# GpSimd's order in the last stage, the drain of attention, and the low parts of the feed-forward's weights: one change to a four-layer conditioned kernel

## Chip, cores and metric

The kernel runs on one core of a Trainium2 chip. Times are microseconds of device time. The kernel before was run three times; its time is their median. A profiled execution of it, taken by the hardware profiler, gives the page and the trace; its own time lies a little beside the median, and both are given below. A core has five engines that work at the same time, each through its own queue of instructions in a fixed order: TensorE (matmuls; PE, with PEld for its weight loads), VectorE (DVE), ScalarE (ACT), GpSimd (POOL) and SyncE (SP), which here only issues DMAs. GpSimd issues some DMAs too.

## The reference

`x` is 64 samples of 64 tokens with 256 features, `cond` 64 samples of 64 features. Four layers follow one another:

```python
# L0: norm with a scale from cond, gated up projection, int8 values times ternary weights
h = x * (scale(cond) * rsqrt(mean(x*x) + 1e-6))
val, gate = split(h @ up_w.T)                      # 2 x 1024
x = x + act_quant(val * gelu(gate)) @ weight_quant(down_w).T
# L1: attention (16 heads of 16), then SwiGLU; gamma, beta, alpha are made from cond
x = x + a_alpha * attention(a_gamma * rms(x) + a_beta)
n = f_gamma * rms(x) + f_beta
x = x + f_alpha * ((silu(n @ gate_w.T) * (n @ hidden_w.T)) @ out_w.T + out_b)
# L2: layernorm, with tanh of a projection of cond added
x = (layernorm(x) * weight + bias + tanh(lin(cond))) * weight + bias
# L3: a bottleneck of 128 whose two weight matrices are made for each sample from cond
Wd_b = Wd + 0.1 * (cond @ Wdd.T + bdd);  Wu_b = Wu + 0.1 * (cond @ Wdu.T + bdu)
x = x + relu(x @ Wd_b.T + bd) @ Wu_b.T + bu
```

The change touches the feed-forward of L1 (SwiGLU), L2 and L3, and the way into them from the attention.

## The kernel before

**Stages.** The 4096 tokens are cut into 8 blocks (`NBLK`) of 512 tokens, 8 samples each. Stage 1 (about 20 to 272 us of the trace) does L0 for all blocks and makes the per-sample parts of L3's weights, which GpSimd's DMAs store in DRAM (`s1d`, `s2d`). Stage 2 (273 to 465 us) does the attention in 16 half blocks `w` and stores its result `x2` in DRAM. Stage 3 does the feed-forward, L2 and L3 in one loop (lines 1003 to 1028). Between stages 2 and 3 lies a stretch written out by hand, the drain of attention (lines 971 to 991): the last half block's weighing and projection among the first products of the feed-forward.

**Products in parts.** A product in fp32 is done as three fp32r matmuls (`mm3`, lines 83 to 85): high part by high part, high by low, low by high. The high part is a rounded copy by ScalarE; the low part is the value minus the high part, by VectorE or GpSimd. Weights are taken apart as well: a `Splitter` (lines 168 to 189) loads a slice, ScalarE copies the high part (L187), VectorE subtracts (L188). One of them takes the attention's weights in stage 1, a second one, made at line 896, takes the feed-forward's in stage 2, 16 slices in all, one or two for each `w` from 1 to 13 (lines 953 to 956).

**The loop of stage 3.** Step `n = 8i + f` handles slice `f` of the hidden layer (128 of 1024) for block `i`:
- `f_inner(n)`: TensorE's products for gate and hidden values (`gh` banks), Silu by ScalarE (L689), their product `sg` by VectorE (L690);
- `f_parts(n)`: the high part `hhi` by ScalarE (L709), the low part `hlo` by VectorE (L710);
- `f_outer(n-2)`: TensorE's product of slice `n-2` with the output weights, into the `acc` banks;
- at `f == 1`, `f_residual(i-1)` closes the block before: two products with alpha (L734), two sums with `x2` (which holds the bias already), called `fx` in the trace (L737), statistics (L739, L740), the root `rs_ln` on GpSimd (L200, L202) and four scalings on VectorE (L743). Then `f_weights(i-1)` loads the adapters' weights `wd` and `wu` on SyncE's queue (L753, L756) and adds the part that is common to all samples with four GpSimd sums of 128x1024 (L759);
- at `f == 3`, `f_rows(i)` loads alpha and bias rows on SyncE and adds the bias to `fx` with two GpSimd sums (L673); `f_start(i+1)` loads the next block's `x2`, squares it on ScalarE (L209), takes its root `rs_f` on GpSimd (L200, L202), and normalises it with four VectorE instructions (L223) into `xnf`;
- at `f` 5 and 6, `f_norm(i+1)`: TensorE transposes (L230), VectorE multiplies by gamma (L233, `xg`), GpSimd adds beta (L234), ScalarE copies the high part (`xhf`), GpSimd subtracts for the low part (L217, `xlf`);
- at `f` 4 to 7, `f_adapt` (transposes L769, L2's weights L770), `f_down` (L780) and `f_up` (L794, L796) do L2's end and L3 for block `i-1`.

`f_last` (from L799) does the last block's end in two halves.

**What sets the order.** Up to line 992, `manual_schedule` (line 92) holds TensorE, ScalarE, VectorE and GpSimd to the order of the source. At 992 `ordered.close()` ends that, and from there the language's scheduler decides where an instruction stands in its engine's queue. SyncE's queue is not in the manual list. Buffers set the rest: two banks in PSUM for `mm`, two for `acc`, four for `gh`; two `st` tiles (used by `sg` and by the Splitter), three `oh`/`ol` tiles (`hhi`/`hlo`), four each of `wd` and `wu`, one of the alpha rows.

**The drain.** Slices 0 to 2 of block 0 were multiplied during the attention's last two half blocks and parked in SBUF (`f_keep`, `room`, lines 693 to 697). In the drain `f_kept(n)` (line 699) applies Silu (L701) and the product, `f_parts` takes the parts, and `f_outer(0)` to `f_outer(3)` use them.

Of the kernel before, what the change touches and what calls it, by code (L numbers as in the profile page):

```python
# [8 lines left out]
F32 = mybir.dt.float32  # L9
# [8 lines left out]
P = 128  # L18
# [18 lines left out]
def tile_kernel(ctx: ExitStack, tc, xT, x, condT, cw, upT, downT, qkvT, woT, ghT, outT_w,  # L37
# [130 lines left out]
    class Splitter:  # L168


        def __init__(self, *jobs):
            self.todo = [(hi, lo, src.rearrange("(c p) n -> p c n", p=P), c, slice(j, j + step))
                         for hi, lo, src, kc, n, step in jobs for c in range(kc) for j in range(0, n, step)]
            self.there = []
# [9 lines left out]
        def turn(self):  # L184
            if self.there:
                hi, lo, st = self.there.pop(0)
                nc.scalar.copy(hi, st)  # L187
                nc.vector.tensor_tensor(lo, st, hi.bitcast(F32), ALU.subtract)  # L188
            self.load()

    def two(pool, name, kc, n):
# [402 lines left out]
    def a_weigh(w):  # L594

        i, tp = w // 2, w % 2
        pool = pools["b"]
        U = units.pop(w)
        pts, rp = U["pts"], U["rp"]
        po, vb = bank("po"), ablk[i]["vb"]  # L600
        for u in range(2):
            for m in range(2):
                for h in range(2):
                    o = (2 * u + m) * P + h * 64
                    for j in range(4):
                        nc.tensor.matmul(po[32 * j:32 * (j + 1), o:o + 64],  # L606
                                         lhsT=vb[:, 2 * tp + u, h, 4 * m + j, :], rhs=pts[j // 2][:, j % 2, o:o + 64],
                                         start=True, stop=True, tile_position=(0, 32 * j))
        of = pool.tile([P, 512], F32, tag="of", bufs=1, name=f"of{w}")
        nc.scalar.copy(of, po)  # L610
        pr = bank("mm")
        for a in range(4):
            nc.tensor.transpose(pr[:, a * P:(a + 1) * P], rp[:, 8 * a:8 * a + 8].rearrange("p h d -> p (h d)"), ident)
        nc.vector.tensor_tensor(of, of, pr, ALU.mult)
        units[w, "f"] = of
# [50 lines left out]
    def f_rows(i):  # L666

        fblk[i]["at"] = load_rows(1, "alpha", i)
        ab = load_rows(2, "ab", i)
        x2 = fblk[i]["x2"]  # L670
        for tp in range(TT // 2):
            s = slice(2 * tp, 2 * tp + 2)
            nc.gpsimd.tensor_tensor(x2[:, s], x2[:, s], ab[:, s], ALU.add)  # L673
# [12 lines left out]
    def f_inner(n):  # L686
        pg, pv = f_products(n)
        sg = main.tile([P, T], F32, tag="st", bufs=2, name=f"sg{n}")
        nc.scalar.activation(sg, pg, AF.Silu)  # L689
        nc.vector.tensor_tensor(sg, pv, sg, ALU.mult)  # L690
        return sg

    def f_keep(n):
# [2 lines left out]
        nc.scalar.copy(room[n][:, 0], pg)  # L696
        nc.vector.tensor_copy(room[n][:, 1], pv)

    def f_kept(n):
        g, v = room[n][:, 0], room[n][:, 1]  # L700
        nc.scalar.activation(g, g, AF.Silu)  # L701
        nc.vector.tensor_tensor(g, v, g, ALU.mult)
        return g

    def f_parts(n, sg):
        pool = pools["b"]
        h_hi = pool.tile([P, T], F32R, tag="oh", bufs=3, name=f"hhi{n}")
        h_lo = pool.tile([P, T], F32R, tag="ol", bufs=3, name=f"hlo{n}")
        nc.scalar.copy(h_hi, sg)  # L709
        nc.vector.tensor_tensor(h_lo, sg, h_hi.bitcast(F32), ALU.subtract)  # L710
        fun[n] = (h_hi, h_lo)

    def f_outer(n):
        i, f = divmod(n, 8)
        h_hi, h_lo = fun.pop(n)
        wout = pools["wout"]
        if f == 0:
            fblk[i]["acc"] = [bank("acc") for _ in range(2)]
        acc = fblk[i]["acc"]
        for t in range(TT):  # L720
            ts = slice(t * P, (t + 1) * P)
            mm3(acc[t // 2][:, (t % 2) * D:(t % 2 + 1) * D], (h_hi[:, ts], h_lo[:, ts]),
                (wout[0][:, f], wout[1][:, f]), f == 0 and t % 2 == 0, f == 7 and t % 2 == 1)
# [22 lines left out]
    def f_weights(i):  # L746
        pool = pools["c"]
        fblk[i]["wd"], fblk[i]["wu"] = [], []
        for k in range(2):
            bs = slice(i * BB + 4 * k, i * BB + 4 * k + 4)  # L750
            wd = pool.tile([P, 4, 2, BN], F32, tag="wd", bufs=4, name=f"wd{i}_{k}")
            for c in range(2):
                nc.sync.dma_start(out=wd[:, :, c, :], in_=s1d[c, bs].rearrange("b d n -> d b n"))  # L753
            wu = pool.tile([P, 4, D], F32, tag="wu", bufs=4, name=f"wu{i}_{k}")
            for s in range(2):
                nc.sync.dma_start(out=wu[s * 64:(s + 1) * 64], in_=s2d[s, bs].rearrange("b n d -> n b d"))  # L756
            bias = pools["bias"]
            for w, row in ((wd.rearrange("p b c n -> p b (c n)"), bias[:, 0]), (wu, bias[:, 1])):
                nc.gpsimd.tensor_tensor(w, w, row.unsqueeze(1).broadcast_to([P, 4, D]), ALU.add)  # L759
            fblk[i]["wd"].append(wd)  # L760
            fblk[i]["wu"].append(wu)

    def f_adapt(i, c):
        B = fblk[i]
# [97 lines left out]

    vx = pools["vx"] = pools["kv"].tile([P, TT, 2, 8, 32], F32, name="vx")
    nc.gpsimd.memset(vx, 0.0)
    splits = Splitter((qkv[0], qkv[1], qkvT, 2, 3 * D, 256), (wo[0], wo[1], woT, 2, D, 256))

    hooks = {3: [cond_load], 4: [cond_rest], 7: [splits.load]}
    for n in range(8, 16):
# [24 lines left out]
    pools["tags"] = dict(S=1, mm=4)  # L893
    pools["gh"] = two(fw, "gh", 2, 2 * FF)
    pools["wout"] = two(fw, "wout", 8, D)
    splits = Splitter((*pools["gh"], ghT, 2, 2 * FF, 512), (*pools["wout"], outT_w, 8, D, 256))
    splits.load()
    N = NBLK * 8
    W = 2 * NBLK
# [14 lines left out]
    for w in range(W):  # L914
        i, tp = divmod(w, 2)
        todo = [lambda k=k: a_ahead(i + 1, k) for k in ((2, 3, 4) if tp == 0 else (5, 6, 7))]
        if i + 1 == NBLK:
            if tp == 0:
                room = rooms()
            todo = [lambda: f_keep(0), lambda: f_keep(1)] if tp == 0 else [lambda: f_keep(2), lambda: a_turn(w, 0)]  # L920
            todo.append(lambda: None)
        a_score(w)
        a_shift(w, 0)
        if w > 0:
            a_weigh(w - 1)
        a_shift(w, 1)
        if tp == 1:
            ablk[i]["at"] = load_rows(0, "alpha", i)
            if i + 3 < NBLK:
                a_load(i + 3)  # L930
            elif i + 3 == NBLK:
                f_load(0)
        if tp == 0:
            if i + 2 < NBLK:
                a_scale(i + 2)
            elif i + 2 == NBLK:
                f_scale(0)
        a_exp(w, 0)
        if w > 0:
            a_parts(w - 1)  # L940
        todo[0]()
        a_sum(w, 0)
        todo[1]()
        a_exp(w, 1)
        todo[2]()
        for rest in late:
            rest()
        late = []
        if tp == 0 and i + 2 <= NBLK:
            late = [a_norm_turn(i + 2, c) for c in range(2)]  # L950
        a_sum(w, 1)
        if w > 0:
            a_project(w - 1)
        a_recip(w)
        if 1 <= w < 14:
            splits.turn()
            if w % 4 == 0:
                splits.turn()
        if w < W - 1:
            a_turn(w, 0)  # L960
            a_turn(w, 1)
            a_rows(w)
        if tp == 1:
            if i + 3 < NBLK:
                a_begin(i + 3)
            elif i + 3 == NBLK:
                f_begin(0)
# [4 lines left out]
    a_rows(W - 1)  # L972
    s0 = f_kept(0)
    f_parts(0, s0)
    s1 = f_kept(1)
    f_parts(1, s1)
    s3 = f_inner(3)
    a_weigh(W - 1)
    s2 = f_kept(2)
    a_parts(W - 1)  # L980
    f_outer(0)
    f_outer(1)
    f_parts(2, s2)
    f_parts(3, s3)
    a_project(W - 1)
    f_rows(0)
    f_start(1)
    s4 = f_inner(4)
    f_outer(2)
    f_parts(4, s4)  # L990
    f_outer(3)
    ordered.close()
    side.close()


# [7 lines left out]
    for n in range(5, N + 2):  # L1003
        i, f = divmod(n, 8)
        if n < N:
            f_parts(n, f_inner(n))
        if n == N:
            f_weights(NBLK - 1)
        if n > 5:
            f_outer(n - 2)  # L1010
        if f == 1 and 0 < i < NBLK:
            f_residual(i - 1)
            f_weights(i - 1)
        if i == NBLK:
            continue
        if f == 3:
            f_rows(i)
            if i + 1 < NBLK:
                f_start(i + 1)
        if i + 1 < NBLK and f in (5, 6):  # L1020
            f_norm(i + 1, f - 5)
        if i > 0:
            if f in (4, 5):
                f_adapt(i - 1, f - 4)
            if f == 6 and i + 1 < NBLK:
                f_down(i - 1)
            if f == 7 and i + 1 < NBLK:
                f_up(i - 1)
    f_last(NBLK - 1)


# [53 lines left out]
```

## Time and profile before

| what | value |
|---|---|
| median of 3 runs (lowest, highest) | 799.27 us (797.81, 801.54) |
| the profiled execution's own time | 794.82 us |
| its span, first to last instruction | 793.0 us |
| mean granted TensorE clock | 0.994 |
| TensorE busy, 20 to 272 us (stage 1) | 250.16 of 252.00 us |
| TensorE busy, 273 to 465 us (stage 2) | 178.93 of 192.00 us |
| TensorE busy, 465 to 495 us (block 0 of stage 3) | 29.37 of 30.00 us |
| TensorE busy, 495 to 515 us | 14.39 of 20.00 us |
| TensorE busy, 515 to 790 us (rest of stage 3) | 268.70 of 275.00 us |
| GpSimd busy, 495 to 515 us; 515 to 790 us | 19.83 of 20.00 us; 124.38 of 275.00 us |

How to read it: busy times add the lengths of an engine's instructions in a stretch; what an engine lacks to the stretch's length is time in which it waited or issued. The clock is the share of full speed that TensorE was granted. In lines of the trace, `L710 DVE TENSOR_TENSOR hlo<-sg,hhi 128x512` is an instruction of VectorE from line 710 that writes a tile `hlo` of 128 partitions by 512 elements from `sg` and `hhi`; `x3` after it says that three such instructions are summed in the line. A timeline line begins with the start (us) and the busy time (us). A bracket such as `[2.09 <-DVE xnf L223]` tells how long the engine waited before and for what. A wait is read "TensorE's `acc` (L85) waited for VectorE's `hlo`: us in total, times, longest".

### The profile page before, as it was taken

What the parts mean: (1) busy time and instruction counts of PE and PEld (TensorE: products, weight loads), DVE (VectorE), ACT (ScalarE), POOL (GpSimd) and SP (SyncE); (2) the same over time, 40 slices, a digit from 0 to 9 for tenths busy, and PEclk for the clock granted to TensorE, in tenths of its full rate; (3) what the DMA queues carried; (4) which work ended last, traced back from release to release, by engine and by line L of the source; (5) the groups of instructions that cost most, each with busy time, mean ns of one, the idle gap of its engine ahead of it and who ended that gap; (6) DMA issues with size and microseconds to landing.
All of it is one profiled execution on the core that took longest, in us unless ns stands there. A gap on an engine that the chain in (4) does not pass through costs nothing.

```text
span 793.0 us, 17333 instructions
## 1 busy us (share of the span) xinstructions
PE 752.4 (95%) x7014; PEld 618.7 (78%) x7014; DVE 575.8 (73%) x926; ACT 371.3 (47%) x758; POOL 326.2 (41%) x304
## 2 busy tenths in 40 slices
PE   4999999999999989989999999699999999999996
PEld 3677767767767878878878888588888888888885
DVE  4678778768678699999989866455565657565755
ACT  4624354344354588788777653233333332333130
POOL 4312132132135335554544426945454545454500
PEclk9999999999999999999999999989999999999999
DMA  9977898997875856544454229425252626250501
GB/s 322 291 191 229 202 255 247 240 223 248 236 193 154 169 122 151 122 119 115 135 148 114 74 64 242 101 69 145 67 148 56 157 61 153 59 155 18 144 1 55
DMA packets 117136, 118.87 MB, mean 150 GB/s; under 512 B 39568, under 2 KB 100624, under 8 KB 117056
## 3 DMA queue, kind: packets, MB, share of 16 engines
q1 hardware_dynamic: 109024, 91.35, 47.0%
q0 software_dynamic: 7488, 25.37, 8.8%
q8 instruction: 55, 0.90, 0.5%
q10 hardware_dynamic: 544, 1.05, 0.4%
q14 instruction: 25, 0.20, 0.1%
HBM read 71.41 MB, written 29.56 MB: 127 GB/s over the span
## 4 chain that ended last, share of the span: by engine, by line
PE 79%; DVE 8%; DMA 4%; issue 3%; POOL 3%; ACT 1%; SPq 1%; POOLq 0%; DVEq 0%; ACTq 0%
PE mm L83 10%; PE mm L85 10%; PE mm L84 10%; PE gh L83 6%; PE gh L85 6%; PE gh L84 6%; PE mm L269 4%; PE acc L85 4%; PE mm L396 4%; PE acc L84 3%; PE acc L83 3%; PE mm L587 2%; PE mm L230 2%; PE mm L606 2%; PE mm L794 2%
## 5 line engine op out<-in xcount | busy, mean ns | idle before, releaser
L83 PE MATMUL mm<-up,xhl 128*128 128x512 f32 x256 | 106.6, 416 | 2.2 <-ACT xhl L216 2.2
L84 PE MATMUL mm<-up,xhl 128*128 128x512 f32 x256 | 102.6, 401 | 0.5 <-DVE up L304 0.5
L85 PE MATMUL mm<-up,xll 128*128 128x512 f32 x256 | 102.4, 400 | 0.0
L83 PE MATMUL gh<-xhf,gh 128*128 128x512 f32 x244 | 98.9, 406 | 0.0
L84 PE MATMUL gh<-xlf,gh 128*128 128x512 f32 x244 | 95.7, 392 | 0.5 <-POOL xlf L217 0.5
L85 PE MATMUL gh<-xhf,gh 128*128 128x512 f32 x244 | 95.9, 393 | 0.0
L709 ACT CAST hhi<-sg 128x512 fp32r<-128x512 f32 x61 | 37.9, 621 | 119.5 <-DVE sg L690 119.5
L690 DVE TENSOR_TENSOR sg<-gh,sg 128x512 f32<-128x512 f32 x61 | 41.7, 684 | 66.3 <-PE gh L85 61.3
L370 ACT ACTIVATE g<-mm,rs_l 128x512 f32<-128x512 f32 x64 | 44.0, 689 | 87.0 <-PE mm L85 63.3
L85 PE MATMUL acc<-wout,hlo 128*128 128x256 f32 x256 | 74.1, 290 | 8.1 <-DVE hlo L710 8.0
L371 DVE SCALAR_TENSOR_TENSOR h<-mm,rs_l,g 128x512 f32<-128x512 f32 x64 | 47.6, 746 | 42.5 <-PE mm L85 41.2
L83 PE MATMUL acc<-wout,hhi 128*128 128x256 f32 x256 | 73.5, 287 | 1.6 <-ACT hhi L709 1.6
L710 DVE TENSOR_TENSOR hlo<-sg,hhi 128x512 fp32r<-128x512 f32 x61 | 55.5, 910 | 26.6 <-ACT hhi L709 26.3
L84 PE MATMUL acc<-wout,hhi 128*128 128x256 f32 x256 | 73.5, 287 | 0.0
L83 PEld LDWEIGHTS mm<-up,xhl 128*128 128x128 f32 x256 | 48.9, 191 | 25.4 <-DVE am L379 4.9
L234 POOL TENSOR_TENSOR xg<-xg,cv 128x512 f32<-128x512 f32 x32 | 33.1, 1042 | 80.5 <-DVE xg L233 80.5
L689 ACT ACTIVATE sg<-gh 128x512 f32<-128x512 f32 x61 | 36.3, 595 | 51.6 <-PE gh L85 51.6
L85 PEld LDWEIGHTS mm<-up,xll 128*128 128x128 f32 x256 | 48.7, 190 | 12.1 <-DVE xll L217 0.5
L84 PEld LDWEIGHTS mm<-up,xhl 128*128 128x128 f32 x256 | 48.8, 191 | 11.4 <-DVE up L304 1.2
L85 PEld LDWEIGHTS acc<-wout,hlo 128*128 128x128 f32 x256 | 49.8, 195 | 8.7 <-DVE hlo L710 8.7
L85 PEld LDWEIGHTS gh<-xhf,gh 128*128 128x128 f32 x244 | 45.9, 188 | 10.6
L83 PEld LDWEIGHTS acc<-wout,hhi 128*128 128x128 f32 x256 | 49.6, 194 | 4.2 <-ACT hhi L709 1.9
(191 smaller groups left out, 1875.1 us busy)
## 6 DMA issues: line engine op xcount, KB each, us to landing
gt<-in_g SPq DMA_DIRECT2D x32, 512.0 KB, 5.9
rows<-alphad SPq DMA_DIRECT2D x48, 256.0 KB, 4.0
s1d<-stg POOLq DMA_DIRECT2D x32, 256.0 KB, 6.6
s2d<-stg POOLq DMA_DIRECT2D x32, 256.0 KB, 6.4
vb<-vx SPq DMA_DIRECT2D x32, 256.0 KB, 4.7
wd<-s1d SPq DMA_DIRECT2D x32, 256.0 KB, 4.1
wu<-s2d SPq DMA_DIRECT2D x32, 256.0 KB, 5.6
xf<-in_xT SPq DMA_DIRECT2D x8, 512.0 KB, 4.0
```

What stands on the lines that cost most here:

```text
L83: nc.tensor.matmul(out, lhsT=l[0], rhs=r[0], start=first, stop=False)
L84: nc.tensor.matmul(out, lhsT=l[0], rhs=r[1], start=False, stop=False)
L85: nc.tensor.matmul(out, lhsT=l[1], rhs=r[0], start=False, stop=last)
L234: nc.gpsimd.tensor_tensor(b3(xg), b3(xg), bc(vb, c, i), ALU.add)
L269: nc.tensor.matmul(pb[s][c * 64:(c + 1) * 64], lhsT=gl[h], rhs=gt[h, c * GC:(c + 1) * GC], start=True, stop=True, tile_position=(64 * s, 6 ...
L370: nc.scalar.activation(g, pg, AF.Gelu, scale=rs[:, t:t + 1])
L371: nc.vector.scalar_tensor_tensor(h[:, ch * 512:(ch + 1) * 512], pv, rs[:, t:t + 1], g, ALU.mult, ALU.mult)
L396: nc.tensor.matmul(py[:, :D], lhsT=qt[:, f, :], rhs=wq[:, f, :], start=f == 0, stop=f == 7)
L689: nc.scalar.activation(sg, pg, AF.Silu)
L690: nc.vector.tensor_tensor(sg, pv, sg, ALU.mult)
L709: nc.scalar.copy(h_hi, sg)
L710: nc.vector.tensor_tensor(h_lo, sg, h_hi.bitcast(F32), ALU.subtract)
```

## The change

It has three parts.
- The `Splitter` takes the engine for its subtraction: VectorE for the attention's weights as before, GpSimd for the feed-forward's 16 slices.
- In the drain, Silu of the parked slices is a function of its own, `f_silu`, and stands earlier: that of slice 0 already in the attention's last half block, in place of a step that did nothing there. `f_inner(4)` comes between `f_outer(0)` and `f_outer(1)`, `f_parts(2)` before `f_outer(1)`, and `f_rows(0)` and `f_start(1)` before the last projection.
- In stage 3 GpSimd is held to the order of the source (a second `manual_schedule`, of GpSimd alone). `f_weights` only loads; the four sums are in `f_common`, two for `wd` after `f_residual(i-1)` at `f == 1`, two for `wu` at `f == 3`, after `f_start(i+1)` and `f_rows(i)`, which have changed places. The last block's weights are loaded at `f == 3` of that block and summed behind the loop's last product.

In the built program GpSimd's queue in the middle of a block of stage 3 is now: `rs_ln` of block i-1, two `wd` sums, `rs_f` of block i+1, two `fx` sums of block i, two `wu` sums, then `xg` and `xlf` twice. VectorE's queue has lost the 16 subtractions of stage 2 and is otherwise the same outside the drain; TensorE's differs in the drain alone, where the products of slice 4 come earlier. Lines of the kernel after are a few higher than before (L759 is L769 there, L710 is L713, L223 is L224).

```diff
@@ -168,7 +168,8 @@
     class Splitter:
 
 
-        def __init__(self, *jobs):
+        def __init__(self, eng, *jobs):
+            self.eng = eng
             self.todo = [(hi, lo, src.rearrange("(c p) n -> p c n", p=P), c, slice(j, j + step))
                          for hi, lo, src, kc, n, step in jobs for c in range(kc) for j in range(0, n, step)]
             self.there = []
@@ -185,7 +186,7 @@
             if self.there:
                 hi, lo, st = self.there.pop(0)
                 nc.scalar.copy(hi, st)
-                nc.vector.tensor_tensor(lo, st, hi.bitcast(F32), ALU.subtract)
+                self.eng.tensor_tensor(lo, st, hi.bitcast(F32), ALU.subtract)
             self.load()
 
     def two(pool, name, kc, n):
@@ -696,9 +697,11 @@
         nc.scalar.copy(room[n][:, 0], pg)
         nc.vector.tensor_copy(room[n][:, 1], pv)
 
+    def f_silu(n):
+        nc.scalar.activation(room[n][:, 0], room[n][:, 0], AF.Silu)
+
     def f_kept(n):
         g, v = room[n][:, 0], room[n][:, 1]
-        nc.scalar.activation(g, g, AF.Silu)
         nc.vector.tensor_tensor(g, v, g, ALU.mult)
         return g
 
@@ -754,11 +757,16 @@
             wu = pool.tile([P, 4, D], F32, tag="wu", bufs=4, name=f"wu{i}_{k}")
             for s in range(2):
                 nc.sync.dma_start(out=wu[s * 64:(s + 1) * 64], in_=s2d[s, bs].rearrange("b n d -> n b d"))
-            bias = pools["bias"]
-            for w, row in ((wd.rearrange("p b c n -> p b (c n)"), bias[:, 0]), (wu, bias[:, 1])):
-                nc.gpsimd.tensor_tensor(w, w, row.unsqueeze(1).broadcast_to([P, 4, D]), ALU.add)
             fblk[i]["wd"].append(wd)
             fblk[i]["wu"].append(wu)
+
+    def f_common(i, which):
+
+        for w in fblk[i][which]:
+            if which == "wd":
+                w = w.rearrange("p b c n -> p b (c n)")
+            row = pools["bias"][:, int(which == "wu")]
+            nc.gpsimd.tensor_tensor(w, w, row.unsqueeze(1).broadcast_to([P, 4, D]), ALU.add)
 
     def f_adapt(i, c):
         B = fblk[i]
@@ -862,7 +870,7 @@
 
     vx = pools["vx"] = pools["kv"].tile([P, TT, 2, 8, 32], F32, name="vx")
     nc.gpsimd.memset(vx, 0.0)
-    splits = Splitter((qkv[0], qkv[1], qkvT, 2, 3 * D, 256), (wo[0], wo[1], woT, 2, D, 256))
+    splits = Splitter(nc.vector, (qkv[0], qkv[1], qkvT, 2, 3 * D, 256), (wo[0], wo[1], woT, 2, D, 256))
 
     hooks = {3: [cond_load], 4: [cond_rest], 7: [splits.load]}
     for n in range(8, 16):
@@ -893,7 +901,7 @@
     pools["tags"] = dict(S=1, mm=4)
     pools["gh"] = two(fw, "gh", 2, 2 * FF)
     pools["wout"] = two(fw, "wout", 8, D)
-    splits = Splitter((*pools["gh"], ghT, 2, 2 * FF, 512), (*pools["wout"], outT_w, 8, D, 256))
+    splits = Splitter(nc.gpsimd, (*pools["gh"], ghT, 2, 2 * FF, 512), (*pools["wout"], outT_w, 8, D, 256))
     splits.load()
     N = NBLK * 8
     W = 2 * NBLK
@@ -918,7 +926,7 @@
             if tp == 0:
                 room = rooms()
             todo = [lambda: f_keep(0), lambda: f_keep(1)] if tp == 0 else [lambda: f_keep(2), lambda: a_turn(w, 0)]
-            todo.append(lambda: None)
+            todo.append((lambda: None) if tp == 0 else (lambda: f_silu(0)))
         a_score(w)
         a_shift(w, 0)
         if w > 0:
@@ -972,24 +980,27 @@
     a_rows(W - 1)
     s0 = f_kept(0)
     f_parts(0, s0)
+    f_silu(1)
     s1 = f_kept(1)
     f_parts(1, s1)
     s3 = f_inner(3)
     a_weigh(W - 1)
+    f_silu(2)
     s2 = f_kept(2)
     a_parts(W - 1)
     f_outer(0)
+    s4 = f_inner(4)
+    f_parts(2, s2)
     f_outer(1)
-    f_parts(2, s2)
     f_parts(3, s3)
-    a_project(W - 1)
     f_rows(0)
     f_start(1)
-    s4 = f_inner(4)
+    a_project(W - 1)
     f_outer(2)
     f_parts(4, s4)
     f_outer(3)
     ordered.close()
+    ordered.enter_context(tc.manual_schedule(engines={mybir.EngineType.Pool}))
     side.close()
 
 
@@ -1005,18 +1016,24 @@
         if n < N:
             f_parts(n, f_inner(n))
         if n == N:
-            f_weights(NBLK - 1)
+            f_common(NBLK - 1, "wd")
+            f_common(NBLK - 1, "wu")
         if n > 5:
             f_outer(n - 2)
         if f == 1 and 0 < i < NBLK:
             f_residual(i - 1)
             f_weights(i - 1)
+            f_common(i - 1, "wd")
         if i == NBLK:
             continue
         if f == 3:
-            f_rows(i)
             if i + 1 < NBLK:
                 f_start(i + 1)
+            f_rows(i)
+            if i > 0:
+                f_common(i - 1, "wu")
+            if i + 1 == NBLK:
+                f_weights(i)
         if i + 1 < NBLK and f in (5, 6):
             f_norm(i + 1, f - 5)
         if i > 0:
@@ -1027,6 +1044,7 @@
             if f == 7 and i + 1 < NBLK:
                 f_up(i - 1)
     f_last(NBLK - 1)
+    ordered.close()
 
 
 def kernel(x, cond_256, L0_cond_norm_w, L0_cond_up_w, L0_cond_down_w, L1_cond_attn_gamma_w,
```

## The prediction

> **What bounds the kernel now.** I read the page first (busy share, slices), then TensorE's waits in the last stage, then GpSimd and VectorE there in order of time.
>
> ```profile
> span 793.0 us, 17333 instructions
> PE 752.4 (95%) x7014; PEld 618.7 (78%) x7014; DVE 575.8 (73%) x926; ACT 371.3 (47%) x758; POOL 326.2 (41%) x304
> PE   4999999999999989989999999699999999999996
> ```
>
> TensorE is the bound: only start, end and one slice (495 to 515 us) are well below full. Its waits from 480 us on:
>
> ```profile
> PE acc L85 <- DVE hlo L710: 7.8, 1, 7.8
> ```
>
> One wait of 7.8 us. GpSimd's timeline shows where it comes from:
>
> ```profile
> 504.39 2.40 POOL L759 TENSOR_TENSOR wd<-wd,bias 128x1024 f32<-128x1024 f32 x1
> ...
> 511.42 2.34 POOL L759 TENSOR_TENSOR wu<-wu,bias 128x1024 f32<-128x1024 f32 x1
> 513.84 0.19 POOL L200 TENSOR_SCALAR ms_ln<-bmv 128x4 f32<-128x4 f32 x1
> 514.12 1.02 POOL L202 TENSOR_TENSOR rs_ln<-ms_ln,nhalf 128x4 f32<-128x4 f32 x1
> ```
>
> VectorE had the variance at 505.3, but the root (L202) stood behind weight sums (L759). Scaling (L743), the low part (L710) and TensorE followed at 515.2, 516.5 and 517.2. Afterwards TensorE ran at half clock. The other blocks have no such hole; stretches of time (PE, PEld, DVE, ACT, POOL busy, clock, DMA):
>
> ```profile
> 514.00:516.00 2.00, 0.00 (x0) 0.50 0.00 0
> ...
> 519.00:520.00 1.00, 1.00 (x7) 0.50 0.08 16
> ...
> 549.00:589.00 40.00, 40.00 (x338) 35.46 (x338) 24.54 (x42) 13.35 (x28) 19.91 (x15) 1.00 0.42 106
> ```
>
> (The first two are of TensorE alone.) So blocks 1 to 7 can only lose. What keeps them full, in the block at 585 us: both roots run back to back, and VectorE's norm (L223) and low part follow soon.
>
> ```profile
> 594.82 1.02 POOL L202 TENSOR_TENSOR rs_ln<-ms_ln,nhalf 128x4 f32<-128x4 f32 x1
> ...
> 595.81 1.16 POOL L202 TENSOR_TENSOR rs_f<-ms_f,nhalf 128x4 f32<-128x4 f32 x1
> 599.07 1.33 POOL L673 TENSOR_TENSOR fx<-fx,rows 128x512 f32<-128x512 f32 x1 [2.09 <-DVE xnf L223]
> ...
> 598.64 1.90 DVE L223 TENSOR_SCALAR xnf<-fx,rs_f 128x256 f32<-128x256 f32 x3
> ...
> 600.47 0.68 DVE L710 TENSOR_TENSOR hlo<-sg,hhi 128x512 fp32r<-128x512 f32 x1
> ...
> 499.28 4.00 DVE L737 TENSOR_TENSOR x<-x,fx 128x512 f32<-128x512 f32 x2
> ...
> 500.98 3.44 POOL L673 TENSOR_TENSOR fx<-fx,rows 128x512 f32<-128x512 f32 x2
> ```
>
> The last two lines show the two engines blocking each other: alone, L737 takes 0.68 and L673 1.30. Singly they ran as L737 499.28 to 501.58 (behind a sum that ended at 501.0), L673 to 502.72, L737 to 503.27, L673 to 504.42: strictly in turn. And of three norms (0.34 us each alone) one took 1.39 beside L673.
>
> [...]the trace has 0.50 from 514 to 520.
>
> **The change part by part.** The sum is made against the profiled execution: 794.8 us, of which the span is 793.0. The median of the runs is 799.3, 4.5 more; I put the changes on the median.
>
> *Hole of block 0.* GpSimd's roots now come ahead of the sums. From the second matmul of the broken group (509.12) to the next products (520.20) are 11.1 us; in a full block the same stretch is 1.7. With rs_ln 1.3 us after the variance (0.19 + 1.02 and gaps), L743 1.3 and L710 0.6, the low part is there 3.2 us after the variance, at 508.5 or sooner, against 509.24 when it is wanted. Gain 9.4, half clock included. Next late is the norm root, below.
>
> *Drain.* TensorE waited 1.9 us for s0's high part (table load 1.28 and Silu at 461.05, behind the last exponentials), then ran 17 matmuls at 0.21 instead of 0.12 us. Outer 0 and 1 plus transposes should end at 465.4 and ended at 469.4. The Silu moved ahead needs only L564's end at 457.1; it delays a copy of ScalarE (L591) from 458.0 to 459.0, whose weighing starts at 461.1. Inner 4 (2.75 us) between outer 0 and 1 covers s1 and s2. Gain 3.9; bounds 2 and 4. f_rows(0) ahead of the projection moves its two sums ahead of one GpSimd add and store (x2d of block 7, wanted 200 us later); its row loads on SyncE still wait for the projection's product (one buffer): nothing. The last block's weight loads now come at f=3: earlier, nothing.
>
> *Low parts on GpSimd (16 of L188).* VectorE loses 8x0.73 + 8x0.60 = 10.6 us. GpSimd gets 8x1.3 + 8x0.7 = 16 us (L217 is the same shape at 1.29), where it is busy about 6 of 12 us; each stands behind the projection's add, ahead of the next root or ol, with 1 to 2 us of slack. In this stage VectorE (11 to 12 of 12) and TensorE are both nearly full; TensorE's waits on VectorE's ax and pts there sum to about 4 us. I take a gain of 2, bounds -1 and 4.
>
> *Source order in blocks 1 to 6.* This is the large term. GpSimd's built order is now: rs_ln, two wd sums, rs_f, two fx adds, two wu sums, then xg and xlf. So between the roots stand two sums, and after rs_f four operations queue without a wait (fx is now the running block's, not the one just normed). VectorE's order is unchanged: variance, L743 x4, hlo(2), norm t0, sg(3), norms t1 to t3, hlo(3), sg(4), hlo(4), L770. TensorE's too: outer(3) wants hlo(3) at 602.75 in the block above, and the transposes after inner(5) want L770's bank (two banks). In that block's clock:
> - the wu sums no longer hold L710 and L737 at 587 to 591: variance at 592.1, not 594.1. rs_ln ends at 593.6;
> - wd 593.6 to 595.9; hlo(2) takes its turn to 596.5 (wanted 598.1); wd to 598.9; rs_f to 600.2;
> - fx to 601.5, t0 to 601.75, then sg(3); fx to 603.05, t1; wu (2.35) to 605.7, t2; wu to 608.3, t3; hlo(3) 608.5 to 609.1.
> TensorE stands until 609.1 instead of going on at 603.0: 6.1 us. sg(4), hhi, hlo(4) and L770 end at 611.9, where the transposes could come at 610.9: 1.0. Together 7.1 a block; 6 blocks norm a next one: +42.6. Without any lock: t0 at 599.7, hlo(3) at 601.9, still in time: 0. Upper bound 7.7 with half clock (10 matmuls at +0.09 after each hole, partly under the 1.0). Behind the waiting L223 on VectorE stand sg(3), hlo(3), L770; ScalarE's hhi(3) and TensorE wait for them. xg, four sums later than before, still makes the next block's first product, since that slides too.
>
> *Block 7* has no next norm; sums meet only hlo and L743: +1 (0 to 7, if L743 takes turns with all of them).
>
> Sum: -9.4 - 3.9 - 2.0 + 42.6 + 1.0 = +28.3, that is 823.1 for the profiled execution and 827.6 on the median; I say 827.
>
> **The rivals.** *Faster, 784:* the queue on GpSimd costs nothing, since VectorE's norms and low parts slip between[...]. Then -15.3 remains. For it: hlo(3) is in time without a lock. Against: L710 took up to 2.65 us and L737 up to 2.64 where sums ran, against 0.69. It decides at about 2.5 us a block; above, the change loses.
> *Near level, 790 to 815:* turns are taken only in part. If t1 to t3 pass together, hlo(3) ends at 606.8 and the loss is 5.7 (819); if fx finds its rows late and the norms go first, only hlo(4) meets a wu sum: 1.7 to 4 a block, 794 to 808.
> *Slower still, 834 or more:* L743 is locked too in block 7, and half clock follows each hole.
> *The change doesn't do what it says:* excluded, the built order has the roots first; it has the second root behind the sums as well.
>
> **How the numbers follow.** Forecast (820 to 833) 0.45; near level 0.23, most of it above; faster 0.22; slower still 0.10. Less than 0.5% (4 us) can't be told from no change. Faster by more: 0.22 and a little of near level, 0.24; same 0.06; slower 0.70. The range from 785 to 836 leaves out about a tenth at each end; the likeliest case alone is 820 to 833.
>
> **What would show it.** Right: no 7.8 us wait at 509 and no half clock at 465; in blocks 1 to 6 a TensorE wait of about 6 us on hlo in every block, a block of about 47 us against the 40 us of the stretch above, and in the norms L223 single ones of 1.4 to 2.6 us beside fx and wu. Wrong: L223 at 0.35 and blocks of 40 us, or TensorE waiting on xlf instead.

## The result, and the profile after

The kernel after takes 823.0 us (median of 4 runs, 820.12 to 825.77) against 800.11 us (four runs, 797.81 to 801.54): 1.029 times as long, interval 1.023 to 1.035. The profiled execution took 825.77 us, its span is 824.0 us.

The page of the kernel after, its first line and TensorE's slices:

```profile
span 824.0 us, 17355 instructions
...
PE   5999999999999999999999997998989798998986
```

The dip of the kernel before (one 6 at 495 to 515 us) is gone; in its place are small dips in every block from 500 us on. TensorE's waits from 273 us to the end (us in total, times, longest):

```profile
PE acc L85 <- DVE hlo L713: 29.5, 14, 4.9
```

The kernel before had two waits for `hlo` in that stretch, of 7.8 and 0.2 us; now there are fourteen that sum to 29.5. The reader can follow one block in two timelines (start, busy time). GpSimd of the kernel after:

```profile
590.74 1.02 POOL L203 TENSOR_TENSOR rs_ln<-ms_ln,nhalf 128x4 f32<-128x4 f32 x1
591.73 4.81 POOL L769 TENSOR_TENSOR wd<-wd,bias 128x1024 f32<-128x1024 f32 x2
...
596.90 1.02 POOL L203 TENSOR_TENSOR rs_f<-ms_f,nhalf 128x4 f32<-128x4 f32 x1
597.89 2.58 POOL L674 TENSOR_TENSOR fx<-fx,rows 128x512 f32<-128x512 f32 x2
600.44 4.80 POOL L769 TENSOR_TENSOR wu<-wu,bias 128x1024 f32<-128x1024 f32 x2
```

and VectorE of the kernel after beside it:

```profile
591.79 5.54 DVE L746 TENSOR_SCALAR x<-x,bmv,rs_ln 128x256 f32<-128x256 f32 x4 [1.42 <-POOL rs_ln L203]
597.25 0.68 DVE L713 TENSOR_TENSOR hlo<-sg,hhi 128x512 fp32r<-128x512 f32 x1
...
599.24 0.68 DVE L691 TENSOR_TENSOR sg<-gh,sg 128x512 f32<-128x512 f32 x1
599.84 5.55 DVE L224 TENSOR_SCALAR xnf<-fx,rs_f 128x256 f32<-128x256 f32 x3
605.31 0.68 DVE L713 TENSOR_TENSOR hlo<-sg,hhi 128x512 fp32r<-128x512 f32 x1
```

and, of the kernel before, the four scalings of the same block:

```profile
595.88 1.39 DVE L743 TENSOR_SCALAR x<-x,bmv,rs_ln 128x256 f32<-128x256 f32 x4 [1.69 <-POOL rs_ln L202]
```

GpSimd's sums take their own time (2.40 and 2.45 us in the lines above; 2.34 in the kernel before at 509.12, with nothing beside it). VectorE's scalings and norms, which read and write SBUF, do not: four scalings (L746) take 5.54 us beside the `wd` sums, where the kernel before had 1.39, and three norms (L224) 5.55 beside `fx` and `wu`; a norm alone takes 0.35. The product `sg` (L691), which reads a PSUM bank, takes its usual 0.68 in the middle of it. TensorE waits for both low parts: the starts of its matmuls stand at 596.87 and then 597.99 (hlo(2)), and at 602.61 and then 606.05 (hlo(3)). Such a hole of 1.1 or 3.4 us, from start to start, has in it the 0.12 us that one of these matmuls takes anyway. Around the second the clock falls, as the stretches of time of TensorE alone show (length, busy time with the number of matmuls, granted clock, DMA share, GB/s):

```profile
603.00:605.00 2.00, 0.00 (x0) 1.00 0.50 112
605.00:607.00 2.00, 0.95 (x4) 0.62 0.00 0
607.00:609.00 2.00, 2.00 (x12) 0.53 0.00 0
...
605.48:608.89 3.41, 2.84 (x13) 0.50 0.00 0
```

The last line begins and ends where the clock changes. In each of blocks 1 to 6 the trace has one such stretch of 3.4 us at half clock.

Cut at the same events in both traces, the time goes as follows (us, from start to start of TensorE's matmuls; "late sums" and "hold" are the first and the eighth experiment below). The events are the first attention score product (L546 before), the last transposes of `rp` (L613), the first transposes of the norm of block 1 (L230), and the first `f_down` product of each block (L780).

| stretch | before | after | late sums | hold |
|---|---|---|---|---|
| attention: first score product to the last of the `rp` transposes | 188.9 | 185.4 | 184.5 | 184.1 |
| drain: from the first of those four `rp` transposes to the transposes for block 1 | 17.3 | 14.3 | 14.2 | 14.3 |
| to `f_down(0)` | 50.7 | 46.4 | 41.2 | 41.8 |
| `f_down(0)` to `f_down(5)`, per block | 39.9 | 46.2 | 39.7 | 39.9 |
| `f_down(5)` to `f_down(6)`, block 7 | 46.1 | 52.8 | 52.8 | 46.1 |
| `f_down(6)` to the last group of products (L854) | 12.7 | 13.6 | 13.6 | 12.7 |

After minus before: -3.5 - 3.0 - 4.3 + 31.5 + 6.7 + 0.9 = +28.3. The 0.9 of the last row is not GpSimd's order: the drain alone (sixth experiment) has 13.6 there too, and the order alone (seventh) 12.7. The first score product came 2.7 us later in the profiled execution of the kernel after (276.3 against 273.6 us), behind a stage that the change does not touch; TensorE ran there at half clock from 55.9 to 62.8 us, which the execution before did not. Together 31.0, which is the difference of the two profiled executions (825.77 - 794.82). The medians differ by 22.9: the profiled execution before is below its median by 5, the one after is the slowest of its four.

### The profile page after: what moved, and what is told of

Read it like the earlier page. It is cut to its first block, busy times and chain, and to the rows that moved or that the text cites. A ratio compares the mean times of both kernels' runs of the same rounds, so it can differ in the third digit from the quotient of the medians.

```text
span 824.0 us, 17355 instructions
## 1 busy us (share of the span) xinstructions
PE 765.0 (93%) x7014; PEld 626.7 (76%) x7014; DVE 607.4 (74%) x910; ACT 370.7 (45%) x758; POOL 330.6 (40%) x320
## 4 chain that ended last, share of the span: by engine, by line
PE 69%; DVE 16%; issue 8%; DMA 3%; ACT 2%; POOL 1%; DVEq 0%; POOLq 0%; SPq 0%
PE mm L83 10%; PE mm L84 10%; PE mm L85 10%; PE gh L83 4%; PE gh L85 4%; PE gh L84 4%; PE mm L270 4%; PE mm L397 3%; DVE x L746 3%; PE acc L85 2%; DVE xnf L224 2%; PE S L547 2%; PE acc L84 2%; PE mm L588 2%; PE acc L83 2%
## 5 line engine op out<-in xcount | busy, mean ns | idle before, releaser
L85 PE MATMUL acc<-wout,hlo 128*128 128x256 f32 x256 | 76.2, 298 | 29.5 <-DVE hlo L713 29.5
L83 PE MATMUL gh<-xhf,gh 128*128 128x512 f32 x244 | 100.4, 411 | 0.0
L85 PE MATMUL gh<-xhf,gh 128*128 128x512 f32 x244 | 96.9, 397 | 0.0
L691 DVE TENSOR_TENSOR sg<-gh,sg 128x512 f32<-128x512 f32 x61 | 41.7, 684 | 66.6 <-PE gh L85 55.9
L713 DVE TENSOR_TENSOR hlo<-sg,hhi 128x512 fp32r<-128x512 f32 x61 | 47.5, 778 | 25.7 <-ACT hhi L712 25.4
L85 PEld LDWEIGHTS gh<-xhf,gh 128*128 128x128 f32 x244 | 46.4, 190 | 10.8
L83 PEld LDWEIGHTS gh<-xhf,gh 128*128 128x128 f32 x244 | 47.1, 193 | 8.9
```

What stands on the lines that cost most here:

```text
L83: nc.tensor.matmul(out, lhsT=l[0], rhs=r[0], start=first, stop=False)
L85: nc.tensor.matmul(out, lhsT=l[1], rhs=r[0], start=False, stop=last)
```

## Experiments

The theory: VectorE's scalings and norms (5.54 us for four scalings beside the `wd` sums, 1.39 in the kernel before) wait for whole sums of GpSimd, so the place of the sums is what costs. The rivals: the second root, which is now late, makes the hole by itself; or something else in the new order.

**1. Late sums.** TensorE's, VectorE's and ScalarE's queues stay as in the kernel after. GpSimd's changes, and on SyncE's queue the loads of `wd` and `wu` move along with their sums.

```diff
...
-        if n == N:
-            f_common(NBLK - 1, "wd")
-            f_common(NBLK - 1, "wu")
...
         if f == 1 and 0 < i < NBLK:
             f_residual(i - 1)
-            f_weights(i - 1)
-            f_common(i - 1, "wd")
...
             f_rows(i)
-            if i > 0:
-                f_common(i - 1, "wu")
-            if i + 1 == NBLK:
-                f_weights(i)
+        if f == 5:
+            f_weights(i)
         if i + 1 < NBLK and f in (5, 6):
             f_norm(i + 1, f - 5)
+        if f == 6:
+            f_common(i, "wd")
+            f_common(i, "wu")
```

> The kernel after, with each block's weights loaded at f == 5 of the same block and its four sums put behind the second xlf (f == 6), where GpSimd stood idle for 17 us; the queues of TensorE, VectorE and ScalarE are the same as in the kernel after. Theory (VectorE's norms and scalings wait for whole sums of GpSimd): no wait of TensorE for hlo above 0.5 us in blocks 1 to 7, blocks of 40 us instead of 46.2, the norms at about 0.35 us apart from those beside fx; 782 to 790 us, 0.977 to 0.988 of the kernel before. Rival (something else in the new order costs the time: rows behind the start of the next block, GpSimd held to source order as such): still 810 us or more.

Measured: 787.1 us (784.68 to 788.94) against 799.67; ratio 0.985, interval 0.981 to 0.989. VectorE's timeline of this kernel in a block:

```profile
576.01 1.39 DVE L746 TENSOR_SCALAR x<-x,bmv,rs_ln 128x256 f32<-128x256 f32 x4 [1.42 <-POOL rs_ln L203]
...
579.82 1.31 DVE L224 TENSOR_SCALAR xnf<-fx,rs_f 128x256 f32<-128x256 f32 x3
```

Scalings and norms take a quarter of the time, blocks 1 to 6 last 39.7 us, and the hole of block 0 stays closed. Moving the four sums (and their loads) gives back the whole loss in these blocks, so the rest of the new order costs nothing there. At their new place the sums still hold a low part up (L713 at 599.04 takes 2.83 us), but TensorE does not wait for it. One thing went against what I expected: a hole of 5.3 us in block 7 was still there. There no next block is normed; GpSimd ran `fx` at 734.90 and the `wd` sums at 737.44, at once after the root, and the four scalings took 7.43 us:

```profile
734.97 7.43 DVE L746 TENSOR_SCALAR x<-x,bmv,rs_ln 128x256 f32<-128x256 f32 x4 [1.42 <-POOL rs_ln L203]
```

**2. Both roots first.** The `wd` sums go behind `rs_f`.

```diff
             f_weights(i - 1)
-            f_common(i - 1, "wd")
...
                 f_start(i + 1)
+            if i > 0:
+                f_common(i - 1, "wd")
             f_rows(i)
```

> The kernel after with the two wd sums behind rs_f instead of ahead of it: both roots first, then wd, fx, wu. Theory (waits for the sums): the scalings get through before the first sum, so the first hole (1.1 us a block) goes, but the norms still meet wd, fx and wu one by one: hlo(3) about 2.5 us earlier than in the kernel after, the second hole about 1 us instead of 3.3; 796 to 806 us. Rival (the late root alone makes the hole): both holes gone, norms at 0.35 us, 782 to 790 us.

Measured: 819.44 us (817.65 to 820.13); ratio 1.024, interval 1.021 to 1.028. Both expectations missed, the rival's by far more. VectorE of this kernel:

```profile
594.00 2.50 DVE L224 TENSOR_SCALAR xnf<-fx,rs_f 128x256 f32<-128x256 f32 x1
...
597.02 4.49 DVE L224 TENSOR_SCALAR xnf<-fx,rs_f 128x256 f32<-128x256 f32 x3
601.43 2.84 DVE L713 TENSOR_TENSOR hlo<-sg,hhi 128x512 fp32r<-128x512 f32 x1
```

The root is there at 593.5, 1.4 us after the first scaling has started instead of 6.1, and the scalings are free (1.39). But the norms wait for `wd`, then for `fx`, and hlo(3) now arrives just as a `wu` sum has begun: 2.84 us instead of 0.68. My figure for the second hole, 1 us, had left that out; it is 2.5, and `hlo(4)` and L778 follow late by 2 more. Four of the five blocks between `f_down(0)` and `f_down(5)` take 44.2 us, 2 less than after; the stretch to `f_down(0)` is 50.9, with a hole of 5.5 us in it. An early root is worth little while the sums stand behind it.

**3. Without the `wu` sums of blocks 0 to 6.** These blocks leave out the common part of the second adapter matrix; loads and all other queues stay.

```diff
             f_rows(i)
-            if i > 0:
-                f_common(i - 1, "wu")
```

> The kernel after without the wu sums of blocks 0 to 6 (the common part of the second adapter matrix is left out for these blocks); rs_f still stands behind the wd sums. Theory: norms t1 to t3 meet nothing after fx, end about 4 us earlier, so the hole of 3.4 us and the pause after it go, the first hole of 1.1 us stays: 788 to 797 us. Rival (the late root alone makes the hole): the root comes at the same time, so the hole stays: 818 to 826 us.

Measured: 795.1 us (792.55 to 797.88); ratio 0.994, interval 0.992 to 0.997. VectorE of this kernel:

```profile
581.42 5.55 DVE L746 TENSOR_SCALAR x<-x,bmv,rs_ln 128x256 f32<-128x256 f32 x4 [1.42 <-POOL rs_ln L203]
...
589.49 1.29 DVE L224 TENSOR_SCALAR xnf<-fx,rs_f 128x256 f32<-128x256 f32 x3
```

The second root ends 6.2 us after the first, 6.2 also in the kernel after, and yet t1 to t3 take 1.29 us instead of 5.55 and the 3.4 us hole is gone. So the late root alone does not make it. The first hole (1.1 to 1.3 us), of the scalings that meet `wd`, is there in blocks 1 to 6, as expected.

**4. Sums in quarters.** Same work, order and place.

```diff
-            nc.gpsimd.tensor_tensor(w, w, row.unsqueeze(1).broadcast_to([P, 4, D]), ALU.add)
+            for b in range(4):
+                nc.gpsimd.tensor_tensor(w[:, b], w[:, b], row, ALU.add)
```

> The kernel after with every sum of 128x1024 cut into four of 128x256: same work, same order, same place. Theory (a VectorE instruction waits for the running GpSimd instruction to end, and then gets its turn): each wait is up to 0.6 us instead of 2.4; the scalings and hlo(2) are in time, the norms t1 to t3 take about 0.7 us each, the 3.4 us hole falls below 1 us: 791 to 802 us although GpSimd works a little longer. Rivals (the two engines share a bandwidth, so that bytes count and not instructions; or the late root): unchanged or slower, 818 to 830 us.

Measured: 809.5 us (807.9 to 811.85); ratio 1.013, interval 1.009 to 1.017: about half of the gain I expected. VectorE of this kernel:

```profile
585.06 3.06 DVE L746 TENSOR_SCALAR x<-x,bmv,rs_ln 128x256 f32<-128x256 f32 x4 [1.42 <-POOL rs_ln L203]
...
592.66 1.37 DVE L224 TENSOR_SCALAR xnf<-fx,rs_f 128x256 f32<-128x256 f32 x1 [3.39 <-POOL rs_f L203]
...
594.55 2.25 DVE L224 TENSOR_SCALAR xnf<-fx,rs_f 128x256 f32<-128x256 f32 x3
```

The waits shrink with the instruction (t1 to t3 0.75 us each instead of 1.85), so what counts is the length of the GpSimd instruction, not the bytes. But the eight quarters of `wd` take 6.25 us where two whole sums took 4.81. More than half of the difference is GpSimd's own, by an estimate from the kernel after: there a whole sum takes 2.40 us, 2.45 when it follows a scaling's turn (594.08) and 2.85 when it follows that of a low part (L713, two inputs of 128x512; 791.27). At these prices the four scalings and the low part that met the quarters make up 0.65, and 5.6 are left for eight quarters, 0.70 each. So the second root comes 7.6 us after the first. Now VectorE does wait for it (3.39 us), with sg(3) behind the first norm, and TensorE waits in turn. The 5 us hole of block 7 is gone.

**5 and 6. The other two parts alone,** on the kernel before: the Splitter's `nc.gpsimd` for the feed-forward's weights, and the drain's new order with `f_silu`.

```diff
...
-    splits = Splitter((*pools["gh"], ghT, 2, 2 * FF, 512), (*pools["wout"], outT_w, 8, D, 256))
+    splits = Splitter(nc.gpsimd, (*pools["gh"], ghT, 2, 2 * FF, 512), (*pools["wout"], outT_w, 8, D, 256))
```

```diff
...
     f_outer(0)
+    s4 = f_inner(4)
+    f_parts(2, s2)
     f_outer(1)
-    f_parts(2, s2)
     f_parts(3, s3)
-    a_project(W - 1)
     f_rows(0)
     f_start(1)
-    s4 = f_inner(4)
+    a_project(W - 1)
...
```

> The kernel before with only the feed-forward weights' low parts on GpSimd. Prediction's step: 2 us less (bounds 4 less to 1 more). The trace of the kernel after has the end of the attention (the last transposes of rp) only 0.8 us earlier than before, so I now expect 0.5 to 1.5 us less, 798 to 800 us: not to be told from no change. Rival (the low parts hold up GpSimd's adds and ol, on which TensorE waits): 1 to 2 us more.

> The kernel before with only the drain rearranged. Prediction's step: 3.9 us less (bounds 2 and 4); the trace of the kernel after has 3.0 less between the last rp transposes and the norm's transposes. Expected 795 to 797.5 us. Rival (the hole of block 0 takes the gain back, because the sums ahead of the root start when their loads land and not when TensorE is done): the hole grows by 3 us and the time stays at 799 to 800.

Measured: low parts 794.12 us (790.79 to 796.0), drain 794.02 us (790.62 to 795.16), both against 798.75; ratio of each 0.994, interval 0.991 to 0.996. The low parts gain 4.6 us, more than either figure I had, and the drain 4.7, a little more than the range I gave. The 0.8 us in that expectation was misread: it compared the absolute time of an event, while the attention of that execution had begun 2.7 us later. From its own start the attention takes 188.9 us before and 183.4 with the low parts on GpSimd. One execution says little about the size: with VectorE's subtractions the attention takes 188.9 to 189.2 us in three traces (before, drain, seventh experiment), with GpSimd's 183.4 to 186.7 in eight, 4.1 less in the mean. The groups of the kernel before in the attention, 280 to 455 us (count, then busy us and mean ns):

```profile
L188 DVE TENSOR_TENSOR gh<-st,gh 128x512 fp32r<-128x512 f32 x8 | 7.5, 944 | 0.0
...
L188 DVE TENSOR_TENSOR wout<-st,wout 128x256 fp32r<-128x256 f32 x8 | 5.7, 735 | 0.0
```

They held VectorE for 13.2 us, in a stretch where it was busy 163.58 of 175 us. Part of that was waiting beside GpSimd: the shortest of each kind take 0.63 and 0.36 us, the longest 1.77 and 1.50, and these two end 0.55 and 0.29 us behind a sum of GpSimd (L639) that was running when they started. The drain does not lose its gain to the hole of block 0: that was 6.6 us there, not longer than 8.1.

**7. GpSimd's order alone,** on the kernel before: of the change, these lines with `f_weights` and `f_common` taken apart, and `f_rows` behind `f_start`.

```diff
     ordered.close()
+    ordered.enter_context(tc.manual_schedule(engines={mybir.EngineType.Pool}))
...
             f_weights(i - 1)
+            f_common(i - 1, "wd")
...
+            if i > 0:
+                f_common(i - 1, "wu")
```

> The kernel before with only the source order of GpSimd in the last stage (f_weights and f_common apart, the roots ahead of the sums). Prediction's steps: 9.4 less at the hole of block 0, 42.6 more in blocks 1 to 6, 1 more in block 7: 34 more than before. From the trace of the kernel after, with 0.8 and 3.0 us of the other two parts taken back: 826 to 830 us. Rival (the parts act on each other; the order alone costs less): below 820 us.

Measured: 831.46 us (828.54 to 833.77); ratio 1.042, interval 1.039 to 1.045: 32.7 us more, against 34 in the prediction's steps; it is 1.5 above the range that I had from the trace of the kernel after. The product of the three ratios, 0.9936 x 0.9936 x 1.042, is 1.029, the ratio of the whole change: the parts add up.

**8 and 9. Block 7,** both on top of late sums. In the eighth a small GpSimd instruction reads the last scaled tile, so that `fx` and the sums start behind the scalings; in the ninth only block 7's sums are in quarters.

```diff
...
+            if i + 1 == NBLK:
+                hold = pools["c"].tile([P, TT], F32, name="hold")
+                nc.gpsimd.tensor_scalar(hold, fblk[i - 1]["x3"][:, TT - 1, :TT], 1.0, 0.0, ALU.mult, ALU.add)
             f_rows(i)
```

```diff
...
+            if i + 1 == NBLK:
+                for b in range(4):
+                    nc.gpsimd.tensor_tensor(w[:, b], w[:, b], row, ALU.add)
+            else:
                 nc.gpsimd.tensor_tensor(w, w, row.unsqueeze(1).broadcast_to([P, 4, D]), ALU.add)
```

> The kernel with late sums, and in block 7 one small GpSimd instruction (128x4) ahead of the two fx sums that reads the last scaled tile, so that fx and the sums start only when VectorE's four scalings are done. In blocks 1 to 6 the second root stood there and gave them that time; in block 7 there is none. Theory (the 5 us hole of block 7 comes of scalings that wait for fx and wd): scalings 1.4 us for four instead of 7.4, the hole of 5.2 us and the half clock after it gone, block 7 about 46 us from one f_down to the next instead of 52.8: 6 to 7 us less than with late sums alone, 0.973 to 0.981 of the kernel before, 778 to 784 us. Rival (the sums then meet the low parts hlo(2) to hlo(4), each of which TensorE needs): a hole of 2 to 4 us somewhat later, 2 us gained or less.

> The kernel with late sums, and block 7's four sums alone cut into quarters of 128x256, in the same place. Theory (a wait lasts as long as the GpSimd instruction that runs): the scalings still meet the two fx sums of 1.3 us and then quarters of 0.6: about 4 us for four instead of 7.4, hlo(2) in time: the hole gone or under 0.5 us: 5 to 7 us less than with late sums alone, 778 to 785 us. Rival (bytes count, not instructions): the hole of 5 us stays, 785 to 789 us.

Measured: hold 777.95 us (776.64 to 779.93), ratio 0.973, interval 0.970 to 0.977; quarters 779.92 us (777.79 to 785.85), ratio 0.977, interval 0.973 to 0.981, both against 798.98. VectorE of the kernel with the hold, and then of the one with quarters, at block 7's scalings:

```profile
737.72 1.38 DVE L746 TENSOR_SCALAR x<-x,bmv,rs_ln 128x256 f32<-128x256 f32 x4 [1.42 <-POOL rs_ln L203]
```

```profile
739.72 4.17 DVE L746 TENSOR_SCALAR x<-x,bmv,rs_ln 128x256 f32<-128x256 f32 x4 [1.42 <-POOL rs_ln L203]
```

The scalings take 1.38 us and 4.17 us where late sums had 7.43, and in both no hole is left in the block. Behind the hold the sums meet low parts instead (L713 at 740.99 takes 1.81), which have that much time to spare: the rival, a hole somewhat later, did not come. The kernel with the hold has the lowest median of all, 2.7% below the kernel before; its interval overlaps that of the quarters, so the two can't be told apart.

## Why the prediction was right, point by point

The direction, the size and the mechanism held: 823.0 us lies in the likeliest case (820 to 833, said 827). The closeness of the total is in good part luck. The cuts of the two profiled executions sum to +28.3, the very figure of the prediction, though two large terms were off by 6 us in opposite directions and three smaller ones by 0.9 to 1.5; the executions as a whole differ by 31.0, the medians by 22.9.

- *Hole of block 0*, -9.4: measured -9.5 (50.7 to 41.2, seen with late sums). In the kernel after 5.2 of it are lost again to block 1's share of the new stalls, as the sum has it.
- *Drain*, -3.9 with bounds 2 and 4: -3.0 in the trace. Alone the drain gave 4.7 on the median, with the hole 1.5 us shorter. Which of its moves gives how much was not separated.
- *Low parts*, -2 with bounds -1 and 4: mis-sized. Measured -3.5 in the kernel after, -5.5 alone in the traces, 4.6 on the median. The step took half of TensorE's waits that name VectorE (about 4 us) without a reason for the half; the gain is about the whole. It also counted 10.6 us of VectorE's time where the trace has 13.2.
- *Blocks 1 to 6*, +42.6: measured +36.7 (5.2 and five times 6.3). The large term is of the right kind, but its parts are not right. The step had the scalings done in 1.3 us and hlo(2) in time: that failed. The first scaling started 60 ns after the first `wd` sum and the four took 5.54 us, which gave the first hole. The step also let every turn of VectorE hold up GpSimd, 14.7 us from the root `rs_ln` to the end of the last `wu` sum. In the trace GpSimd's instructions follow one another with hardly a gap, 13.5 us; the norms and scalings come in at their borders, and hlo(3) ended 15.6 us after the variance and not 17.0. TensorE, held up by the first hole, also wanted it 1.1 us later. So the second hole is 3.3 us and not 6.1, the first 1.0 and not 0 (one matmul's 0.12 taken off). The pause before L777 is 0.8 in three of the five blocks from `f_down(0)` to `f_down(5)` and nothing in the other two, and not 1.0.
- What is left is half clock, which the sum had kept for the upper bound. TensorE's order is the same with late sums, so its starts can be compared one by one: in the stretch at half clock it loses 1.4 us where there is no pause, 1.1 where there is one. The blocks take 45.7 and 46.4 us. With GpSimd's order alone (seventh experiment) one block had the same two holes and full clock throughout, and took 45.4 (matmuls of `acc` 0.12 us apart behind the second hole, at 702.7); another had them 0.21 us apart behind its second hole, with matmuls slowed from 609.8 to 615.5 us, and took 47.1. So half clock added 0.3 to 1.7 us to a block.
- *Block 7*, +1 with bounds 0 and 7: measured +6.7. This is the term that was furthest off for its size. The text named the case (L743 in turns with all the sums) and took it for unlikely. The traces show the scalings at 7.45 us and a hole of 5.2, with half clock after it; the hold removes exactly that.
- *What would show it*: no 7.8 us wait at 509 us and no half clock at 465 (right; the clock is 1.00 from 465 to 469, where the kernel before has 0.50); waits on `hlo` in every block, named as about 6 us (0.8 to 1.0 and 3.2); blocks of about 47 us (46.2); norms of 1.4 to 2.6 us (0.78 to 2.5).
- *The rivals.* "Faster" needed VectorE to slip between the sums, and fell with the first experiment: taking the sums away from it is what makes the kernel faster. "Near level" needed turns taken only in part; its case of 5.7 us a block (819 us) lies above the range that it was given.

That VectorE and GpSimd take turns was shown in the kernel before for L737, the low part (2.64 us, 0.69 alone) and one norm in each of six blocks (1.37 to 1.39 beside L673, 0.34 alone); that it would hold for every norm behind a sum was the author's estimate. The runs bear it out: a scaling that started 60 ns after a sum of 2.40 us took 2.49 (0.40 alone). They add the prices: in the block shown two scalings and two norms pay 2.1 us each, while GpSimd pays 0.05 us for a turn of a scaling or norm (2.45 against 2.40) and 0.45 for one of a low part (2.85, at 791.27 in the kernel after).

What stays open: why the hole of block 0 was 1.5 us shorter with the drain alone was not tried, nor why a hole of the same length is followed by half clock in one block and not in another.

## What to carry to other kernels

When an engine's queue is put into a fixed order, price each instruction not only by what waits behind it but by what runs beside it: here GpSimd's long sums cost nothing next to a VectorE that waits (39.7 us a block with late sums) or reads PSUM (L691 0.68 us inside a sum), and 6.5 us a block (46.2) next to scalings and norms that stand ahead of a low part which TensorE needs. Roots first was right; the sums had to go as well, to a stretch where VectorE has one such instruction at a time and slack behind it (L713 took 2.83 us there, and TensorE did not wait). And check the last iteration by itself: it lacks the work that kept the queue apart in the others (a hole of 5.3 us in block 7 with late sums).

## What the runs showed of the hardware

- A scaling or norm of VectorE that started while a GpSimd sum ran ended 0.15 to 0.16 us behind that sum, a low part 0.55 to 0.56 us (up to 0.64 where less than 0.15 us of the sum was left), in every case after 470 us in the traces of the kernels before and after, however long the sum still had to run (0.05 to 2.35 us). L713 in experiments 1 (599.04) and 8 (740.99) ended about 0.55 us behind `wd` and `fx`. Four scalings took 1.39 us with no sum beside them, 5.54 where two of them met 128x1024 sums (2.49 us each), 3.06 where all four met 128x256 ones (0.82 each). Instructions with a PSUM operand kept their time beside sums: L691 0.68 to 0.69 us in the kernel after, L734 0.68 to 0.69 and L796 0.73 to 0.75 in the kernel before. So did the statistics, though they read and write SBUF: in the kernel before L739 took 0.39 to 0.42 us and L740 0.16 to 0.17 inside sums, as alone.
- Finer instructions were not free for GpSimd: two whole sums took 4.81 us with VectorE's turns between them, eight quarters 6.25 to 6.66; of the 6.25, 5.6 are GpSimd's own by the estimate in the fourth experiment.
- The hole of 3.4 us between two starts on TensorE came with a granted clock of 0.50 for 3.4 us in all of blocks 1 to 6 of the kernel after, but only in four of these six with GpSimd's order alone were the `acc` matmuls behind it slowed (0.21 us apart instead of 0.12). Nor does it take one long hole: in the kernel before the clock was 0.50 from 465.6 to 469.0 us, and in the 3.4 us ahead of that TensorE's longest wait was 1.6 us.
